# Second layer of a two-layer state-space kernel: state sums by fp32 transposes, softplus terms joined on TensorE, seven of 24 C-products on GpSimd

## The chip, the cores and the metric

The kernel runs on one core of one Trainium2 chip. The metric is the device time of a whole execution in microseconds (us); lower is better. Everything is fp32.

## The reference, cut to what matters

Two layers run one after the other on a tensor of 8 images, 192 channels and 64 x 64 pixels. The change touches the second layer alone, a bidirectional Mamba block on 8 sequences of 4096 tokens with 192 channels. It normalises the tokens, runs the function below twice (once on the channels in reverse order, with its own weights), and adds both results to the normalised tokens.

```python
xc, z = split(x @ in_w.T)                    # 384 channels each
xc = silu(causal_conv(xc, 4 taps) + conv_b)
dt, B, C = split(xc @ x_w.T)                 # 12, 16, 16
dt = softplus(dt @ dt_w.T + dt_b)            # 384 channels
A = -exp(A_log)                              # 384 x 16 states
h[t] = exp(dt[t] * A) * h[t-1] + (dt[t] * xc[t]) * B[t]
y[t] = sum over the 16 states of h[t] * C[t]
y = (y + D * xc) * silu(z)
return y @ out_w.T
```

## The kernel before, in words

The second layer works on blocks of 512 tokens. There are 8 sequences of 8 blocks, and each block is passed twice (index `i` 0 and 1, one per Mamba), so there are 128 **passes**. Channels lie on the 128 partitions, in three channel blocks `c`, and tokens on the free axis. The 16 states of a channel block are taken two at a time, so a pass has 24 **groups** (3 channel blocks, 8 groups each), and the main loop (L947) has one **slot** per group. I number slots 0 to 23 within a pass.

A group does this:

- `inputs` (L831, GpSimd): dt * xc times B, for two states, 128 x 1022. It is issued three slots ahead.
- `decays` (L836, ScalarE): two exponentials into a PSUM tile `da`, and a copy of the first column. It is issued two slots ahead. There are two `da` buffers of two banks each.
- `scan` (L845, VectorE): the recurrence as one scan over 1024 elements.
- `keep` (L850, ScalarE): the last state is saved.
- `weigh` (L853): the product with C. It runs on VectorE for most groups (I call these near) and on GpSimd for the groups listed in `FAR` (far). The scan of a far group writes SBUF.
- `sum` (L857, TensorE): two matmuls with the identity add the two states into the PSUM tile `yp` of the channel block, three slots later (near) or four (far). The channels stay on the partitions.

Everything else of a pass is spread over the slots in two lists: `before[n]` is issued ahead of the scan of slot n, `behind[n]` after the decays of slot n. Much of it already belongs to the next pass. `enter` projects the input, `convolve` does the four taps as matmuls with diagonal weights (L695), `gate` projects z (L706), `silu` changes ScalarE's function table twice, `low_rank` computes dt, B and C, `spread` sends B and C by DMA to all partitions. `step` (L736) forms the terms of softplus on ScalarE, in six operations. `refine` (L753) joins them in three GpSimd operations and forms dt * xc in a fourth. `head` (L766) prepares the first column and waits for dt * xc. `gated` (L785) multiplies z by `yp`; `project` (L788) multiplies by the output weights, and `add` (L810) adds the result up.

Each engine issues its instructions strictly in the order in which the program emits them, so an instruction that waits holds up all that stand behind it on its engine. TensorE results outside `yp` go to PSUM tiles of the tag `bank` (L557). There are two of these, and a third result has to wait until the reader of an older one is done. The readers are ScalarE copies and activations, and VectorE for `add` when `i` is 1.

The order in one slot is `before`, `inputs` of slot n+3, `scan`, `sum` of older groups, `weigh`, `keep`, `decays` of slot n+2, `behind` (L947 to L972).

Of the kernel before, what the change touches and what calls it, by code (L numbers as in the profile page):

```python
# [8 lines left out]
F32 = mybir.dt.float32  # L9
# [22 lines left out]
FAR = (0, 12, 15, 20)  # L32
# [507 lines left out]
def kernel(ctx: ExitStack, tc: tile.TileContext, mid, ln, mambas, out):  # L540
# [21 lines left out]
    eps = const.tile([P, 2], F32, name="eps")  # L562
    eps, minus_one = eps[:, 0:1], eps[:, 1:2]
    nc.gpsimd.memset(eps, 1e-5)
    nc.gpsimd.memset(minus_one, -1.0)
# [99 lines left out]
    class Pass:  # L665
# [40 lines left out]
        def gate(self, c):  # L706
            if self.z is None:
                self.z = p2.tile([P, NC, T], F32, tag="z", name=f"z_{self.tag}")
            nc.scalar.copy(self.z[:, c, :], self.in_proj(NC + c))
# [26 lines left out]
        def step(self, c):  # L736


            pd = bank(f"pd_{self.tag}_{c}")
            nc.tensor.matmul(pd, self.m.dt_w[:, c * P : (c + 1) * P], self.dbl[:DTR, :], start=True, stop=True)  # L740
            self.e, self.lg, self.w = (
                p2.tile([P, T], F32, tag=kind, bufs=1, name=f"{kind}_{self.tag}_{c}") for kind in ("e", "lg", "w")
            )
            d = p2.tile([P, T], F32, tag="dt", name=f"dt_{self.tag}_{c}")
            nc.scalar.activation(self.e, pd, AF.Abs, bias=self.m.dt_b[:, c : c + 1])
            nc.scalar.activation(d, pd, AF.Relu, bias=self.m.dt_b[:, c : c + 1])  # L746
            nc.scalar.activation(self.e, self.e, AF.Exp, scale=-1.0)
            nc.scalar.activation(self.lg, self.e, AF.Ln, bias=1.0)
            nc.scalar.activation(self.w, self.e, AF.Identity, bias=1.0)
            nc.scalar.activation(self.w, self.w, AF.Identity, bias=minus_one)  # L750
            self.dt.append(d)

        def refine(self, c, part):  # L753
            d = self.dt[c]
            if part == 0:
                nc.gpsimd.tensor_sub(self.e, self.e, self.w)  # L756
            elif part == 1:
                nc.gpsimd.tensor_add(self.lg, self.lg, self.e)
            elif part == 2:
                nc.gpsimd.tensor_add(d, d, self.lg)  # L760
            else:
                dtx = p2.tile([P, T], F32, tag="dtx", name=f"dtx_{self.tag}_{c}")
                nc.gpsimd.tensor_mul(dtx, d, self.xc[:, c, :])
                self.dtx.append(dtx)

        def head(self, c, part):  # L766


            d, state = self.dt[c], self.m.state[:, c, :]
            if part == 0:  # L770
                first = self.first[c] = p2.tile([P, NS], F32, tag="first", name=f"first_{self.tag}_{c}")
                nc.scalar.activation(first, self.b0, AF.Identity, scale=self.dtx[c][:, 0:1])
                if self.k:
                    self.rest = p2.tile([P, NS], F32, tag="rest", name=f"rest_{self.tag}_{c}")
                    nc.scalar.activation(self.rest, self.m.a[:, c, :], AF.Exp, scale=d[:, 0:1])
                nc.scalar.copy(d[:, 0:1], never)
            elif self.k:
                nc.gpsimd.tensor_mul(self.rest, self.rest, state)
                nc.gpsimd.tensor_add(self.first[c], self.first[c], self.rest)

        def accumulate(self, c):
            self.yp.append(ps.tile([P, T], F32, tag="yp", name=f"yp{c}_{self.tag}"))
            nc.tensor.matmul(self.yp[c], self.m.d_diag[:, c, :], self.xc[:, c, :], start=True, stop=False)

        def gated(self, c):  # L785
            nc.vector.tensor_mul(self.z[:, c, :], self.z[:, c, :], self.yp[c])  # L786

        def project(self, half):  # L788

            self.po = bank(f"po_{self.tag}_{half}", (P, 2, CM))  # L790
            for s in range(2):
                at = slice((2 * half + s) * P, (2 * half + s + 1) * P)
                for c in range(NC):
                    nc.tensor.matmul(
                        self.po[:, s, :],
                        self.z[:, c, at],
                        self.m.out_w[:, c, :],
                        start=(c == 0),
                        stop=(c == NC - 1 and self.i == 1),
                    )  # L800
                for i in range(2 if self.i == 0 else 0):
# [3 lines left out]
                        ident[:KM, :KM],  # L805
                        start=False,
# [13 lines left out]
    class Group:  # L820
# [36 lines left out]
        def sum(self):  # L857
            for n in range(NG):
                stop = self.g == GROUPS - 1 and n == NG - 1
                nc.tensor.matmul(self.p.yp[self.c], ident, self.hs[:, n, :], start=False, stop=stop)  # L860
# [12 lines left out]
    for n, p in enumerate(passes):  # L873
        for c, slot in enumerate((-7, 1, 9)):
# [3 lines left out]
            for part in range(4):  # L878
                at(before, n, slot + 4, p.refine, c, part)
            for part in range(2):  # L880
                at(before, n, slot + 4 + part, p.head, c, part)
        for half, slot in enumerate((5, 10)):
            at(behind, n + 1, slot, p.project, half)
            at(before, n + 1, slot + 2, p.add, half)
# [10 lines left out]
        for c, slot in enumerate((13, 14, 16)):  # L895
            at(before, n - 1, slot, p.gate, c)
# [17 lines left out]
    with tc.manual_schedule():  # L914
# [7 lines left out]
        for c in range(NC):  # L922
            first.enter(c)
            first.convolve(c, range(4))
            first.gate(c)
# [6 lines left out]
        for part in range(4):  # L932
            first.refine(0, part)
# [13 lines left out]
        for n in range(len(before)):  # L947
# [11 lines left out]
            for by, far in ((3, False), (4, True)):  # L959
# [91 lines left out]
```

## Time and profile before

The median of three runs is 16998.13 us (16997.56 to 17017.5). The profiled execution has a span of 16996.8 us from its first to its last instruction; the page gives no other time for it, and the fastest run is 0.8 us above that span.

| stretch | span us | PE busy | DVE busy | ACT busy | POOL busy |
|---|---|---|---|---|---|
| whole execution | 16996.8 | 15880.5 | 15268.1 | 11938.6 | 15164.6 |
| second layer's loop, from its first state sum (6073 to 16990 us) | 10917 | 10116.6 | 10276.0 | 8234.2 | 10435.7 |

PE is TensorE, DVE VectorE, ACT ScalarE, POOL GpSimd. The stretch of the second layer divided by 128 passes is 85.3 us a pass. "Busy" of PE counts pipelined matmuls with modelled ends, so it overstates how full PE is. In the lists of groups, "idle before" is the time in which an engine stood still just ahead of that group, with what ended the wait. In the timeline a bracket holds the same for one row: the idle time and what ended it.

| operation of the second layer | engine | count | mean ns |
|---|---|---|---|
| `inputs` L834 | POOL | 3072 | 2351 |
| `scan` L848, near / far | DVE | 2560 / 512 | 2286 / 2280 |
| `weigh` L855 | DVE / POOL | 2560 / 512 | 1222 / 2353 |
| `sum` L860 (two instructions for each fp32 matmul) | PE | 12288 | 603 |
| `decays` L840 | ACT | 6144 | 691 |
| softplus joins L756, L758, L760 | POOL | 384 each | 1274, 1268, 1268 |
| dt * xc L763 | POOL | 384 | 1268 |
| copy of a 128 x 512 PSUM tile, L709 | ACT | 384 | 579 |

### The profile page before, as it was taken

What the parts mean: (1) busy time and instruction counts of PE and PEld (TensorE: products, weight loads), DVE (VectorE), ACT (ScalarE), POOL (GpSimd) and SP (SyncE); (2) the same over time, 40 slices, a digit from 0 to 9 for tenths busy, and PEclk for the clock granted to TensorE, in tenths of its full rate; (3) what the DMA queues carried; (4) which work ended last, traced back from release to release, by engine and by line L of the source; (5) the groups of instructions that cost most, each with busy time, mean ns of one, the idle gap of its engine ahead of it and who ended that gap; (6) DMA issues with size and microseconds to landing.
All of it is one profiled execution on the core that took longest, in us unless ns stands there. A gap on an engine that the chain in (4) does not pass through costs nothing.

```text
span 16996.8 us, 151143 instructions
## 1 busy us (share of the span) xinstructions
PE 15880.5 (93%) x42192; PEld 6479.2 (38%) x42192; DVE 15268.1 (90%) x14474; ACT 11938.6 (70%) x25451; POOL 15164.6 (89%) x9955
## 2 busy tenths in 40 slices
PE   9999999999999989999999999999999999999998
PEld 2333333333333334444444444444444444444443
DVE  8888888888887779999999999999999999999999
ACT  5656666666666667777777777777777777777777
POOL 7787978778787779999999999999999999999999
PEclk8999999999999999999999999999999999999999
DMA  1001010010100022222222222222222222222222
GB/s 30 24 7 30 1 30 9 22 30 1 30 1 26 3 95 105 105 105 105 104 106 104 106 104 106 104 106 104 106 104 106 104 106 104 106 104 103 106 102 87
DMA packets 695389, 1247.33 MB, mean 73 GB/s; under 512 B 311768, under 2 KB 378672, under 8 KB 694544
## 3 DMA queue, kind: packets, MB, share of 16 engines
q1 hardware_dynamic: 694144, 1237.37, 19.9%
q8 instruction: 335, 5.49, 0.1%
q14 instruction: 510, 4.18, 0.1%
q10 hardware_dynamic: 400, 0.29, 0.0%
HBM read 1178.77 MB, written 58.72 MB: 73 GB/s over the span
## 4 chain that ended last, share of the span: by engine, by line
DVE 26%; ACT 9%; POOL 9%; issue 8%; DMA 8%; PE 5%; SPq 0%; DVEq 0%; POOLq 0%; ACTq 0%
DVE da L848 18%; DMA c_sb<-bc 7%; POOL hs L834 6%; ACT da L840 3%; DVE hs L855 3%; DVE hs L848 3%; PE yp L860 2%; PE dbl_ps L721 1%; POOL hs L855 1%; DVE z L786 1%; DMA b_sb<-bc 1%; ACT xc L713 1%; ACT L713 1%; POOL e L756 1%; ACT xt L650 1%
## 5 line engine op out<-in xcount | busy, mean ns | idle before, releaser
L834 POOL TENSOR_TENSOR hs<-dtx,b_sb 128x1022 f32<-128x1022 f32 x3072 | 7140.1, 2351 | 62.1 <-DMA b_sb<-bc 29.8
L848 DVE TENSOR_TENSOR_SCAN da<-da,hs 128x1024 f32<-128x1024 f32 x2560 | 5852.5, 2286 | 497.0 <-ACT hs L843 462.8
L860 PE MATMUL yp<-hs,ident 128*128 128x512 f32 x12288 | 5764.5, 603 | 47.9 <-POOL hs L855 25.4
L840 ACT ACTIVATE da<-dt,a 128x512 f32<-128x512 f32 x6144 | 4246.7, 691 | 435.9 <-DVE hs L848 257.5
L860 PEld LDWEIGHTS yp<-hs,ident 128*128 128x128 f32 x12288 | 2316.7, 193 | 3058.9 <-issue 2700.9
L855 DVE TENSOR_TENSOR hs<-da,c_sb 128x1024 f32<-128x1024 f32 x2560 | 3129.3, 1222 | 88.4
L237 PE MATMUL g<-xp,w_gate_sb 16*128 16x512 f32 x8640 | 1816.2, 658 | 60.4 <-ACT dx L310 51.6
L851 ACT COPY state<-da 128x2 f32<-128x2 f32 x2560 | 399.4, 156 | 1981.8 <-DVE hs L855 1972.8
L700 PE MATMUL pc<-xr,conv_diag 128*128 128x512 f32 x3072 | 1572.3, 642 | 170.4 <-ACT dt L746 151.9
L678 PE MATMUL pi<-xT,in_w 96*128 96x512 f32 x3072 | 1447.2, 597 | 79.3 <-ACT y L816 36.5
L263 DVE TENSOR_TENSOR q<-g,h 128x512 f32<-128x512 f32 x2016 | 1351.4, 684 | 115.5 <-PE g L237 70.0
L273 PE MATMUL q<-q,ident 128*128 128x512 f32 x2688 | 1333.5, 619 | 0.0
L283 ACT ACTIVATE rc<-g,eps 128x512 f32<-128x512 f32 x672 | 462.0, 687 | 1116.7 <-DVE g L278 1116.7
L313 POOL TENSOR_TENSOR dx<-dx,xc 128x512 f32<-128x512 f32 x768 | 1079.5, 1406 | 156.6 <-ACT dx L310 133.6
L848 DVE TENSOR_TENSOR_SCAN hs<-da,hs 128x1024 f32<-128x1024 f32 x512 | 1167.5, 2280 | 57.2 <-POOL hs L834 57.2
L855 POOL TENSOR_TENSOR hs<-hs,c_sb 128x1024 f32<-128x1024 f32 x512 | 1204.9, 2353 | 1.2 <-ACT state L851 1.2
L267 POOL TENSOR_TENSOR q<-q,q 128x512 f32<-128x512 f32 x672 | 852.7, 1269 | 196.5 <-DVE q L263 190.9
L237 PEld LDWEIGHTS g<-xp,w_gate_sb 16*128 16x128 f32 x8640 | 495.0, 188 | 1304.9 <-DVE q L263 394.3
L700 PEld LDWEIGHTS pc<-xr,conv_diag 128*128 128x128 f32 x3072 | 584.8, 198 | 1029.0 <-issue 660.8
L257 POOL TENSOR_TENSOR lam<-lam,xc 128x512 f32<-128x512 f32 x672 | 942.0, 1402 | 33.3 <-ACT lam L254 33.3
L278 DVE TENSOR_TENSOR g<-g,ab 128x512 f32<-128x512 f32 x1344 | 933.0, 694 | 22.8
L196 DVE SCALAR_TENSOR_TENSOR xc<-pi,dw_sb,xc 128x504 f32<-128x504 f32 (+3 forms) x1152 | 839.5, 736 | 98.4 <-POOL xc L162 63.8
(140 smaller groups left out, 22975.2 us busy)
## 6 DMA issues: line engine op xcount, KB each, us to landing
b_sb<-bc SPq DMA_DIRECT2D x1024, 512.0 KB, 9.0
c_sb<-bc SPq DMA_DIRECT2D x1024, 512.0 KB, 8.9
xin<-in_x_dram SPq DMA_DIRECT2D x192, 384.0 KB, 3.6
mid<-ot SPq DMA_DIRECT2D x128, 192.0 KB, 2.1
xt<-mid SPq DMA_DIRECT2D x64, 384.0 KB, 10.0
out_dram<-y SPq DMA_DIRECT2D x64, 384.0 KB, 2.6
bc<-dbl SPq DMA_DIRECT2D x128, 64.0 KB, 1.6
b<-bc SPq DMA_DIRECT2D x128, 8.0 KB, 7.3
```

The costliest lines, as they stand in the source:

```text
L237: nc.tensor.matmul(dst, self.wg[r, at, self.d, :], flat(self.xp[r, self.j]), start=True, stop=True)
L257: nc.gpsimd.tensor_mul(self.lam if self.j else self.hc, self.lam, direction(self.xc, self.d, self.j))
L263: nc.vector.tensor_mul(self.q[i], rows(self.g[i]), self.h[:, :, i : i + HW])
L273: nc.tensor.matmul(self.sum, ident, flat(term), start=(i == 0), stop=(i == 1))
L313: nc.gpsimd.tensor_mul(self.dx, self.dx, direction(self.xc, self.d, self.j))
L678: nc.tensor.matmul(pi, self.m.in_w[:, i, c * P : (c + 1) * P], self.tokens.xT[:, i, :], start=(i == 0), stop=(i == 1))
L700: nc.tensor.matmul(pc, self.m.conv_w[:, c, t, :], self.xr[c][:, t : t + T], start=(t == 0), stop=(t == 3))
L834: nc.gpsimd.tensor_mul(self.hs[:, :, 1:], dtx, self.p.b_sb[self.g][:, :, 1:])
L840: nc.scalar.activation(self.da[:, n, :], self.p.dt[self.c], AF.Exp, scale=self.p.m.a[:, self.c, at : at + 1])
L848: nc.vector.tensor_tensor_scan(h, da, hs, 0.0, ALU.mult, ALU.add)
L855: engine.tensor_mul(self.hs, self.h, self.p.c_sb[self.g])
L860: nc.tensor.matmul(self.p.yp[self.c], ident, self.hs[:, n, :], start=False, stop=stop)
```

## The change

The state sum turns the layout over. For each of the two states and each 128 tokens, `sum` uses the slice of `hs` as the stationary operand and the identity as the moving one, with the transpose flag, and accumulates in `yp`. So `yp` has tokens on the partitions and channels on the free axis. `gate` and `accumulate` produce z and D * xc in that layout. `gated` multiplies there, and a new part, `turn_back`, transposes z back for `project` and copies it with ScalarE. The normalised tokens that `project` adds use the transpose flag too.

The terms of softplus are no longer added on GpSimd. `join` adds them by four matmuls with the identity into a `bank` tile, and `refine` copies the result to dt with ScalarE before GpSimd forms dt * xc. `step` writes a fourth term `r` and changes a sign. `FAR` has seven slots instead of four. `gate` has four parts (by 128 tokens, 384 wide) at slots 12, 13, 14 and 16 instead of three at 13, 14 and 16, and the first half of `project` moves from slot 5 to 6.

```diff
-FAR = (0, 12, 15, 20)
+FAR = (0, 3, 6, 9, 14, 17, 22)
...
-        def gate(self, c):
+        def gate(self, s):
...
-            nc.scalar.copy(self.z[:, c, :], self.in_proj(NC + c))
+                self.z = p2.tile([P, T // P, CI], F32, tag="z", name=f"z_{self.tag}")
+            pi = bank(f"pz_{self.tag}_{s}", (P, CI))
+            for i in range(2):
+                nc.tensor.matmul(
+                    pi,
+                    self.tokens.xT[:, i, s * P : (s + 1) * P],
+                    self.m.in_w[:, i, CI:],
+                    start=(i == 0),
+                    stop=(i == 1),
+                )
+            nc.scalar.copy(self.z[:, s, :], pi)
...
+            nc.scalar.activation(e, pd, AF.Abs, bias=self.m.dt_b[:, c : c + 1])
+            nc.scalar.activation(r, pd, AF.Relu, bias=self.m.dt_b[:, c : c + 1])
+            nc.scalar.activation(e, e, AF.Exp, scale=-1.0)
+            nc.scalar.activation(lg, e, AF.Ln, bias=1.0)
+            nc.scalar.activation(w, e, AF.Identity, bias=1.0)
+            nc.scalar.activation(w, w, AF.Identity, bias=1.0, scale=-1.0)
+
+        def join(self, c):
+
+            self.pj = bank(f"pj_{self.tag}_{c}")
+            for i, term in enumerate(self.terms):
+                nc.tensor.matmul(self.pj, ident, term, start=(i == 0), stop=(i == 3))
+
+        def refine(self, c):
             d = p2.tile([P, T], F32, tag="dt", name=f"dt_{self.tag}_{c}")
...
+            nc.scalar.copy(d, self.pj)
             self.dt.append(d)
-
-        def refine(self, c, part):
-            d = self.dt[c]
-            if part == 0:
-                nc.gpsimd.tensor_sub(self.e, self.e, self.w)
-            elif part == 1:
-                nc.gpsimd.tensor_add(self.lg, self.lg, self.e)
-            elif part == 2:
-                nc.gpsimd.tensor_add(d, d, self.lg)
-            else:
-                dtx = p2.tile([P, T], F32, tag="dtx", name=f"dtx_{self.tag}_{c}")
-                nc.gpsimd.tensor_mul(dtx, d, self.xc[:, c, :])
-                self.dtx.append(dtx)
+            dtx = p2.tile([P, T], F32, tag="dtx", name=f"dtx_{self.tag}_{c}")
+            nc.gpsimd.tensor_mul(dtx, d, self.xc[:, c, :])
+            self.dtx.append(dtx)
...
         def accumulate(self, c):
-            self.yp.append(ps.tile([P, T], F32, tag="yp", name=f"yp{c}_{self.tag}"))
-            nc.tensor.matmul(self.yp[c], self.m.d_diag[:, c, :], self.xc[:, c, :], start=True, stop=False)
+            self.yp.append(ps.tile([P, T // P, P], F32, tag="yp", name=f"yp{c}_{self.tag}"))
+            for s in range(T // P):
+                nc.tensor.matmul(
+                    self.yp[c][:, s, :],
+                    self.xc[:, c, s * P : (s + 1) * P],
+                    self.m.d_diag[:, c, :],
+                    start=(s == 0),
+                    stop=False,
+                )
...
+        def turn_back(self, c):
+
+            pt = bank(f"pb_{self.tag}_{c}", (P, T // P, P))
+            z = self.z[:, :, c * P : (c + 1) * P]
+            for s in range(T // P):
+                nc.tensor.transpose(pt[:, s, :], z[:, s, :], ident)
+            nc.scalar.copy(z, pt)
...
                         self.tokens.xT[:, i, at],
                         ident[:KM, :KM],
+                        is_transpose=True,
...
         def sum(self):
             for n in range(NG):
-                stop = self.g == GROUPS - 1 and n == NG - 1
-                nc.tensor.matmul(self.p.yp[self.c], ident, self.hs[:, n, :], start=False, stop=stop)
+                for s in range(T // P):
+                    nc.tensor.matmul(
+                        self.p.yp[self.c][:, s, :],
+                        self.hs[:, n, s * P : (s + 1) * P],
+                        ident,
+                        is_transpose=True,
+                        start=False,
+                        stop=(self.g == GROUPS - 1 and n == NG - 1 and s == T // P - 1),
+                    )
...
             at(behind, n, slot, p.step, c)
-            for part in range(4):
-                at(before, n, slot + 4, p.refine, c, part)
+            at(behind, n, slot + 3, p.join, c)
+            at(before, n, slot + 4, p.refine, c)
             for part in range(2):
                 at(before, n, slot + 4 + part, p.head, c, part)
-        for half, slot in enumerate((5, 10)):
+        for c, slot in enumerate((13, 21, 29)):
+            at(behind, n, slot, p.turn_back, c)
+        for half, slot in enumerate((6, 10)):
             at(behind, n + 1, slot, p.project, half)
             at(before, n + 1, slot + 2, p.add, half)
...
-        for c, slot in enumerate((13, 14, 16)):
-            at(before, n - 1, slot, p.gate, c)
+        for s, slot in enumerate((12, 13, 14, 16)):
+            at(before, n - 1, slot, p.gate, s)
...
-            for by, far in ((3, False), (4, True)):
+            for by, far in ((4, True), (3, False)):
```

The parts of the first pass, which stand ahead of the loop, change in the same way.

## The prediction

> **What bounds the kernel now.** I read the page first: in the second layer (the stretch from 6073 to 16990 us, 128 passes of 85.29 us) VectorE and GpSimd are both nearly full. The line gives the stretch, its length, the busy time of PE, PEld, DVE, ACT and POOL, then the granted clock (0.97), the DMA share and GB/s.
>
> ```profile
> 6073.00:16990.00 10917.00, 10116.60 (x25245) 4497.95 (x25246) 10276.04 (x6638) 8234.23 (x18795) 10435.66 (x6263) 0.97 0.27 104
> ```
>
> Per pass that is VectorE 80.3, GpSimd 81.5, ScalarE 64.3. Then VectorE's timeline, to see how a slot is spent and where it stops:
>
> ```profile
> 10010.56 2.29 DVE L848 TENSOR_TENSOR_SCAN da<-da,hs 128x1024 f32<-128x1024 f32 x1
> 10014.02 2.29 DVE L848 TENSOR_TENSOR_SCAN da<-da,hs 128x1024 f32<-128x1024 f32 x1
> ...
> 10036.18 2.28 DVE L848 TENSOR_TENSOR_SCAN hs<-da,hs 128x1024 f32<-128x1024 f32 x1
> 10038.38 2.27 DVE L848 TENSOR_TENSOR_SCAN da<-da,hs 128x1024 f32<-128x1024 f32 x1
> ...
> 10049.17 2.30 DVE L848 TENSOR_TENSOR_SCAN da<-da,hs 128x1024 f32<-128x1024 f32 x1 [1.60 <-ACT hs L843]
> 10058.44 2.30 DVE L848 TENSOR_TENSOR_SCAN da<-da,hs 128x1024 f32<-128x1024 f32 x1 [2.25 <-ACT hs L843]
> ```
>
> A near slot lasts 3.46 us (first two rows), a far one 2.20 (next two). So VectorE needs 20 x 3.46 + 4 x 2.20 + 3.1 (gated, add, statistics) = 81.1 a pass; the rest is waiting, and the list of waits says for whom:
>
> ```profile
> DVE da L848 <- ACT hs L843: 462.8, 238, 2.6
> PEld pi L678 <- ACT y L816: 72.1, 62, 2.1
> PEld pi L678 <- ACT xc L704: 70.7, 64, 5.4
> ```
>
> First row: VectorE waits for ScalarE's decays, 462.8 / 128 = 3.62 us a pass. The next two tell what decides this case: TensorE stands still until ScalarE has read an older `bank` tile. With two such tiles the order of TensorE and ScalarE is one chain.
>
> **What is saved.** Three more products leave VectorE: 3 x (3.46 - 2.20) = 3.78 us a pass. GpSimd loses nine joins at 1.27 = 11.4 and gains three products at 2.353 = 7.1: 81.5 falls to 77.1. TensorE's matmuls of 512 columns follow each other at 0.43 us (four in 1.72). A transpose is much shorter:
>
> ```profile
> 10064.88 0.60 PE L657 MATMUL pt<-ident,xt 128*96 128x128 f32 x4
> 10065.32 1.88 PE L860 MATMUL yp<-hs,ident 128*128 128x512 f32 x4
> ```
>
> Four take 0.44, 0.11 each, with weights of 96 columns. Loads of 128 columns (L802) follow at 0.125 (four from 10097.72 to 10098.22), so 0.11 to 0.13; I take 0.11, since the sums move 128 columns as L657 does. The sums go from 96 x 0.43 = 41.3 to 192 x 0.11 = 21.1; `join` adds 24 x 0.43 = 10.3, `turn_back` 12 x 0.11 = 1.3, `accumulate` 24 x 0.17 (rate of L794's matmuls) - 6 x 0.43 = 1.5. Net -7 a pass: by these rates TensorE has (96 + 24 + 24 + 18) x 0.43 for sums, convolutions, projections and the rest of 512 columns, 24 x 0.17 for L794 and about 2 for L802 and L657, 75.8 before and 69 after (73 at 0.13). ScalarE gains three copies of dt and three of z at 0.58: 64.3 to 67.8. `gate` is as long as before (16 x 0.32 against 12 x 0.43), and the shorter transposes of L802 are worth under 1 us off the path. `project`'s first half and its add move by one slot together, so its bank is held no longer; the new order of far and near sums costs TensorE nothing, since both operands are there. The dropped constant is one memset of 0.1 us. If ScalarE's waits stayed at 3.62, a pass would take 81.5.
>
> **What it adds: waits.** ScalarE has a narrow margin. Per slot it needs 1.63 (keep and decays, 10042.42 to 10044.05), and its lateness shows on VectorE once the two-slot lead is used up. Behind a far slot the lead is 1.26 shorter. `join` (3.44 us of TensorE) stands in front of the second half of a convolution in slots 4 and 12, and ScalarE must wait for that convolution (L704), then for the copy of dt, then for a round trip to GpSimd (dtx 1.27 + 0.1; `head` needs it), before its next decays. Before, GpSimd did the joins in advance, and L772's wait for dtx was 107 us in all. I follow each place by rows of this trace.
>
> *Slots 11 to 15*, from the end of product 11. VectorE reaches scan 15 after add 0.54 + 3.46 + 3.46 + 2.20 = 9.7. ScalarE: decays 13 until 1.6. The first `gate`, now in slot 12, finds one bank held by the half-done convolution and the other by `project`, so it starts after the add (0.54), ends at 2.1, is copied by 2.6. `scale` (1.86) and decays 14 take ScalarE to 6.1. `join` needs the gate's bank: 2.6 + 3.44, then convolution 1.72 + 0.2 pipeline = 8.0. L704 to 8.6, dt copy 9.2, dtx 10.5, head 11.2, next gate copy 11.7, decays 15 done at 13.3. Wait 3.7. When `i` is 1 the add is a ScalarE copy, the gate is copied by 4.2, decays 15 are done at 14.9 against 9.1: 5.8. Mean 4.7; before: none here.
>
> *Slots 15 to 18*, from scan 15: copies 1.0, decays 16 at 2.6, decays 17 after product 15 at 5.1, gate and silu block 6.05 (10050.56 to 10056.61), decays 18 at 12.8. VectorE, slot 17 being far, is there at 9.1. Wait 3.7.
>
> *Slots 1 to 4*: decays 4 ended 12.7 after scan 0 began (10079.46 to 10092.17) behind `step`; VectorE now arrives at 11.8. Wait 0.9.
>
> *Slots 4 to 7*, from scan 4: L704 frees a bank at 0.6, `join` and convolution end at 6.0, L704 6.6, dt copy 7.2, dtx 8.6, head 9.2, decays 7 at 10.9. VectorE: 9.1. Wait 1.8.
>
> *Slots 20 to 23*: `join` is done in time; decays 22, turn, copy, dtx, head and decays 23 are 6.5 against 5.7, without the turn 5.8. Mean wait 0.5.
>
> Sum 4.7 + 3.7 + 0.9 + 1.8 + 0.5 = 11.6 in place of 3.62. The old 1.60 wait (scan 16) goes, with slot 15 no longer far; the silu wait grows. **A pass: 85.29 - 3.78 - 3.62 + 11.6 = 89.5**, +4.2, over 128 passes +540 us. On the span of 16996.8 that is 17,537; the runs lie about 1 us above the span, so **17,540 us**. What hides the cheap edits is the waiting itself: GpSimd (77) and TensorE are off this path, and GpSimd's three extra products run inside its own waits for the dt copy. Without that cover GpSimd's balance is 7.1 - 11.4 = -4.3, still a gain. DMA: no transfer is added; c_sb tiles of groups read by GpSimd come free one slot later, with 9 us to land (page, part 6) and six slots to spare.
>
> Bounds: each wait is a chain of measured pieces, but an engine's lead can shorten it. If every join is done when ScalarE arrives, only round trips and the far slots' shorter lead stay (about 6 us of waits, 84 a pass, 16,830). If pieces slip by another slot's ScalarE work in two places, +3.3: 17,960. This case's own range is 17,200 to 17,900.
>
> **A rule against the change.** The trace shows the clock falling after idle time:
>
> ```profile
> 10053.98 4.46 PE L721 MATMUL dbl_ps<-xc,x_w 128*44 128x512 f32 x6 [2.80 <-ACT xc L713]
> ```
>
> Six matmuls take 4.46 where 6 x 0.43 + 0.16 = 2.7 would do. In the eight transposes per two passes the trace cannot show what a long stretch of transposes does to the clock. The Trainium skill ("TensorE: Matmul & The Clock Gate", Part 4) says that transposes don't count as activity in the way matmuls do, so that the full clock isn't reached among them. By that rule slots 18, 19 and 21 to 23, which now hold hardly anything else, would run at half clock, and the estimate would be that of the second rival; by the 0.97 of the row above, nothing is added.
>
> **Rivals.** *Covered, faster.* TensorE leads ScalarE enough that joins are ready, and the balance of VectorE and GpSimd decides. For it: both were full, both are relieved, and `PE z L786` type waits are small (46 us). Against: the two-bank waits above. It decides if the waits are under 7.4 a pass (3.62 + 3.78). At 3.6 to 6.7 a pass takes 81.5 to 84.6: 16,510 to 16,910, middle 16,700. *Cold clock.* The joins in slots 4, 12 and 20 run at 0.86 a matmul, as the later ones of L721 did (weights loaded at 10055.68 and 10056.54): 3.4 more in each, two of them uncovered, with half of the convolutions: about +5 a pass, 18,180. It needs a clock clearly under 0.9 in the stage. *The transposes do not come out short* (two instructions each, 0.22, so that `sum` doesn't do what it says): 192 x 0.22 = 42 instead of 21, TensorE 90 a pass, a bound of its own beside the forecast's 89.5, some 17,600. The rows of L657 (512 instructions for 64 x 8 transposes) speak against it; it is counted in the forecast's range.
>
> **Chances.** Forecast 0.60, covered 0.27, near no change 0.05 (waits close to 7.4), cold clock 0.08. A measurement of this kernel can tell about 0.2%. Faster is the covered case, 0.27; same 0.05; slower 0.68. The range leaves out 0.1 on each side: the low end lies inside the covered case at 16,620, the high end at the slipped chain, 17,960.
>
> **What would show it.** VectorE's wait for L843 grows from 463 to about 1,480 us and falls on scans 4, 7, 15 and 18, each behind a far slot; ScalarE waits for TensorE at the convolution's activation in slots 4 and 12 and for dtx three times a pass; VectorE busy in the stage falls by 480, GpSimd by about 560; transposes at 0.11. Wrong, if waits stay near 463: then the joins were ahead of ScalarE, and the bank chain is the step that failed. Wrong in another way, if the granted clock drops below 0.9.

## The result and the profile after

The changed kernel takes 17868.1 us (median of four runs, 17853.87 to 17870.83), against 17003.23 us before on the same chip (four runs). The ratio is 1.0506, with a 95% interval of 1.0494 to 1.0519: slower by 5%. The forecast of 17,540 us had the sign and the chain of waits that makes the loss; the time lies 328 us above it, 2.6 us a pass.

The line for the second layer's stretch has the same columns as before: from and to, length, busy time of PE, PEld, DVE, ACT and POOL, then clock, DMA share and GB/s.

```profile
6073.00:17860.00 11787.00, 9665.10 (x44425) 6161.20 (x44426) 9870.44 (x6261) 8543.42 (x19695) 9998.48 (x5499) 0.92 0.26 96
```

The stretch is 870 us longer, and yet VectorE works 406 us less and GpSimd 437 us less. So no engine has become the bound by its work. The clock fell from 0.97 to 0.92. The list of waits of the stretch says who stands still for whom (time in all, times, longest):

```profile
engine line waited for: us in total, times, longest us
POOL dtx L770 <- ACT dt L767: 1666.9, 380, 11.3
...
DVE da L872 <- ACT hs L867: 940.7, 378, 8.6
DVE da L872 <- POOL rest L785: 691.8, 113, 8.9
ACT xc L702 <- PE pc L698: 640.2, 253, 6.8
...
ACT first L779 <- POOL dtx L770: 528.1, 382, 2.4
```

VectorE waits for decays in two rows (the second names a GpSimd operation that was done just before the decays it really waits for): 940.7 + 691.8 = 1632 us, where it had been 463 (a smaller row, put down to ScalarE's copy of the state as at scan 10 below, grew from 34 to 113). The other rows are the links in front of it. ScalarE waits for a convolution that stands behind a join, GpSimd for the dt that ScalarE copies from the join, and ScalarE again for GpSimd's product. VectorE's timeline shows two of its stops in a pass with `i` = 1, scans 10 and 15, each behind a far scan (`hs<-da,hs`):

```profile
12091.23 2.28 DVE L872 TENSOR_TENSOR_SCAN hs<-da,hs 128x1024 f32<-128x1024 f32 x1
12095.16 2.30 DVE L872 TENSOR_TENSOR_SCAN da<-da,hs 128x1024 f32<-128x1024 f32 x1 [1.65 <-ACT state L875]
...
12109.54 2.28 DVE L872 TENSOR_TENSOR_SCAN hs<-da,hs 128x1024 f32<-128x1024 f32 x1
12120.37 2.30 DVE L872 TENSOR_TENSOR_SCAN da<-da,hs 128x1024 f32<-128x1024 f32 x1 [8.55 <-ACT hs L867]
```

From the same records I took VectorE's idle time ahead of each scan, as a mean over passes 5 to 125:

| scan | forecast | measured, i = 0 | i = 1 | mean |
|---|---|---|---|---|
| 4 | 0.9 | 0.14 | 1.07 | 0.6 |
| 7 | 1.8 | 1.85 | 1.86 | 1.9 |
| 10 | 0 | 0.13 | 1.65 | 0.9 |
| 15 | 4.7 (3.7 and 5.8) | 3.72 | 8.73 | 6.2 |
| 18 | 3.7 | 3.63 | 3.65 | 3.6 |
| 23 | 0.5 | 1.67 | 0.35 | 1.0 |
| sum | 11.6 | | | 14.3 |

By the trace, a pass takes 92.19 us from scan to scan (85.39 before). The forecast's sum with the measured waits gives 85.39 - 3.78 - 3.92 + 14.3 = 92.0, so nearly the whole miss of 2.6 us a pass is in this column, and most of it in scan 15 when `i` is 1 (2.9 in half of the passes) and in scan 10.

The timeline around that stop, with the rows of the chain alone:

```profile
12104.36 0.47 ACT L840 COPY y<-po 128x384 f32<-128x384 f32 x1
...
12104.88 1.63 PE L710 MATMUL pz<-in_w,xT 96*128 96x384 f32 x4 [3.45 <-ACT y L840]
...
12107.08 2.08 PE L763 MATMUL pj<-r,ident 128*128 128x512 f32 x2 [0.57 <-ACT state L875]
...
12108.95 1.91 PE L763 MATMUL pj<-e,ident 128*128 128x512 f32 x2
...
12110.65 1.92 PE L763 MATMUL pj<-lg,ident 128*128 128x512 f32 x2
...
12112.36 1.38 PE L763 MATMUL pj<-w,ident 128*128 128x512 f32 x2
...
12115.49 0.69 ACT L702 ACTIVATE xc<-pc,vec_sb 128x512 f32<-128x512 f32 x1 [6.84 <-PE pc L698]
12116.08 0.58 ACT L767 COPY dt<-pj 128x512 f32<-128x512 f32 x1
...
12116.73 1.26 POOL L770 TENSOR_TENSOR dtx<-dt,xc 128x512 f32<-128x512 f32 x1 [11.29 <-ACT dt L767]
...
12118.03 0.31 ACT L779 ACTIVATE first<-b,dtx 128x16 f32<-128x16 f32 x1 [1.37 <-POOL dtx L770]
```

This is the forecast's chain link by link: add, gate, join, convolution, activation, dt, dtx, head. Only one link has another length. The terms of the join start 1.87, 1.70 and 1.71 apart, that is 0.86 an instruction and not 0.43. TensorE had stood still for 3.45 us at the gate just before; whether that is the cause is tested below. When `i` is 0, 61 of 64 of these joins go at 0.44 an instruction, and the wait is the forecast's 3.7.

### The profile page after: what moved, and what is told of

Its sections match the earlier page's. It is cut to its first block, busy times and chain, and to the rows that moved or that the text cites. A ratio compares the mean times of both kernels' runs of the same rounds, so it can differ in the third digit from the quotient of the medians.

```text
span 17867.8 us, 187845 instructions
## 1 busy us (share of the span) xinstructions
PE 15441.3 (86%) x61392; PEld 8143.5 (46%) x61392; DVE 14857.0 (83%) x14090; ACT 12245.6 (69%) x26347; POOL 14723.1 (82%) x9186
## 4 chain that ended last, share of the span: by engine, by line
POOL 34%; DVE 12%; issue 9%; ACT 5%; DMA 4%; PE 1%; SPq 0%; POOLq 0%; DVEq 0%; ACTq 0%
POOL hs L858 25%; POOL hs L879 7%; DVE da L872 6%; DMA c_sb<-bc 4%; DVE hs L872 3%; ACT da L864 2%; DVE hs L879 2%; POOL dtx L770 2%; ACT e L752 0%; ACT r L753 0%; ACT e L754 0%; PE pc L698 0%; ACT xc L721 0%; ACT z L722 0%; PE po L499 0%
## 5 line engine op out<-in xcount | busy, mean ns | idle before, releaser
L858 POOL TENSOR_TENSOR hs<-dtx,b_sb 128x1022 f32<-128x1022 f32 x3072 | 7282.2, 2395 | 32.0 <-DMA c_sb<-bc 1.5
L872 DVE TENSOR_TENSOR_SCAN da<-da,hs 128x1024 f32<-128x1024 f32 x2176 | 4985.3, 2291 | 1809.7 <-ACT hs L867 943.7
L884 PEld LDWEIGHTS yp<-ident,hs 128*128 128x128 f32 x24576 | 2954.6, 147 | 803.2 <-issue 491.6
L884 PE MATMUL yp<-ident,hs 128*128 128x128 f32 x24576 | 3185.1, 283 | 44.6 <-POOL hs L879 26.0
L879 DVE TENSOR_TENSOR hs<-da,c_sb 128x1024 f32<-128x1024 f32 x2176 | 2661.3, 1223 | 86.8
L879 POOL TENSOR_TENSOR hs<-hs,c_sb 128x1024 f32<-128x1024 f32 x896 | 2120.7, 2367 | 15.9 <-ACT state L875 15.9
L872 DVE TENSOR_TENSOR_SCAN hs<-da,hs 128x1024 f32<-128x1024 f32 x896 | 2042.2, 2279 | 60.2 <-POOL hs L858 54.8
L770 POOL TENSOR_TENSOR dtx<-dt,xc 128x512 f32<-128x512 f32 x384 | 487.3, 1269 | 1706.4 <-ACT dt L767 1706.4
L875 ACT COPY state<-da 128x2 f32<-128x2 f32 x2176 | 338.2, 155 | 1261.2 <-DVE hs L879 1252.7
L710 PE MATMUL pz<-in_w,xT 96*128 96x384 f32 x2048 | 820.2, 525 | 401.6 <-ACT y L840 220.4
L817 PE MATMUL po<-out_w,z 128*128 128x192 f32 x3072 | 726.6, 381 | 400.4 <-ACT z L809 400.4
L676 PE MATMUL pi<-xT,in_w 96*128 96x512 f32 x1536 | 758.7, 617 | 278.1 <-ACT z L809 210.2
```

The costliest lines, as they stand in the source:

```text
L858: nc.gpsimd.tensor_mul(self.hs[:, :, 1:], dtx, self.p.b_sb[self.g][:, :, 1:])
L872: nc.vector.tensor_tensor_scan(h, da, hs, 0.0, ALU.mult, ALU.add)
L879: engine.tensor_mul(self.hs, self.h, self.p.c_sb[self.g])
L884: nc.tensor.matmul(self.p.yp[self.c][:, s, :], self.hs[:, n, s * P : (s + 1) * P], ident, is_transpose=True, start=False, stop=(self.g == ...
```

## The experiments

Waits are again the mean idle time of VectorE ahead of a scan, and "a pass" is the mean distance of scan 0 from pass to pass. Ratios are against the kernel before on the same chip, which took 17,000 to 17,004 us (median) on each of them.

### Three parts alone

**Seven far groups alone**, in the kernel before.

```diff
-FAR = (0, 12, 15, 20)
+FAR = (0, 3, 6, 9, 14, 17, 22)
...
-            for by, far in ((3, False), (4, True)):
+            for by, far in ((4, True), (3, False)):
```

> The kernel before with only the list of far groups changed to the seven of the change (and far sums issued ahead of near ones, so that the last sum of a channel stays last). Three theories. CHAIN: the time of the change was lost because the join of softplus stands on TensorE and waits for one of two bank tiles, and ScalarE for it; then seven far products with the joins still on GpSimd show no wait at scans 4, 7 and 15 behind ScalarE's L702-like activation. What is left is GpSimd, 81.5 + 7.1 = 88.6 us a pass, which is now the bound, and the wait of scan 18 for silu, 3.6: about 89 a pass, 17,450. FAR: the seven far groups alone bring the loss; then 92 a pass, 17,850, with waits of scans 15 and 18 for ScalarE as after the change. CLOCK: transposes lower the clock; here there are none in the sums, so the granted clock stays at 0.96 to 0.97, and the time is GpSimd's, 17,450.

17635.95 us, ratio 1.0373 (1.0357 to 1.0388); 90.33 a pass.

```profile
6073.00:17640.00 11567.00, 10441.15 (x25260) 4664.12 (x25260) 9870.95 (x6263) 8191.90 (x18801) 11324.28 (x6650) 0.93 0.26 98
```

The line has the columns of before; GpSimd (the last busy time) works 11324 / 128 = 88.5 of 90.3 us: it is the bound, as CHAIN said, though the time is 1% over CHAIN's. Its lateness shows in ScalarE's wait for dtx, 964 us (102 before). Scans 7 and 15 wait too (2.8 and 3.2), and 4 and 10 a little (0.6 and 0.8), which CHAIN did not expect; the 964 us point to the same round trip, with GpSimd's own joins in place of the join on TensorE. The clock is 0.93, where CLOCK had 0.96 to 0.97: a fall of that size comes without one transposed sum.

**Transposed sums alone**: the kernel after, with the softplus terms joined on GpSimd as before and four far groups.

```diff
-            at(behind, n, slot + 3, p.join, c)
-            at(before, n, slot + 4, p.refine, c)
+            for part in range(4):
+                at(before, n, slot + 4, p.refine, c, part)
...
-FAR = (0, 3, 6, 9, 14, 17, 22)
+FAR = (0, 12, 15, 20)
```

> The kernel after with the softplus joins back on GpSimd and the four far groups of before: the transposed sums alone (with the turn-back of z and the gates in four pieces). CHAIN: no join on TensorE, so no wait at scans 4, 7 and 15 beyond 1 us; the waits of before at 16 and 18 stay, with up to 1 us more at 15 from the gate that stands in slot 12: 85.4 to 87 a pass, 17,000 to 17,200. CLOCK: the short transposes leave TensorE idle or uncounted for most of the time, the granted clock falls to 0.93 as after the change, every matmul piece on the path doubles at times, and the time is 17,300 or more. FAR: as before, 17,000.

17057.86 us, ratio 1.0033 (1.0020 to 1.0045); 85.81 a pass.

```profile
6073.00:17050.00 10977.00, 8536.65 (x41364) 5813.95 (x41365) 10300.32 (x6641) 8444.68 (x19312) 10555.75 (x6264) 0.88 0.28 103
```

PE's busy time falls by 1580 us, and the time hardly moves: TensorE was off the path. The wait of scan 16 shrinks from 1.60 to 0.2, and 0.4 to 0.9 come at 7, 14 and 15; CHAIN had only the one at 15. The clock is 0.88, lower than in any other kernel here, for 0.3% of the time. So CLOCK, as a loss everywhere, is out: here a mean granted clock says nothing, since TensorE has slack.

**Sums and joins on TensorE, four far groups.**

```diff
-FAR = (0, 3, 6, 9, 14, 17, 22)
+FAR = (0, 12, 15, 20)
```

> The kernel after with the four far groups of before: transposed sums and joins on TensorE, no further product on GpSimd. CHAIN: VectorE works 3.8 us a pass more than after the change, the waits at scans 4, 7, 10 and 23 (4.3 in all) go, because no far slot shortens the lead there, those at 15 (3.7 and 8.7) and 18 (3.6) stay: about 91 a pass, 17,750. FAR: the joins cost nothing by themselves, the waits fall back to about 4 a pass: 85.4, 17,000. CLOCK: as after the change less the far part, granted clock 0.93, about 88 a pass.

17830.89 us, ratio 1.0486 (1.0470 to 1.0502); 91.92 a pass, near CHAIN's 91. Scan 15 waits 5.7 and 7.5 (CHAIN: 3.7 and 8.7), scan 18 2.2, scan 14 1.4, which CHAIN did not have, and 4, 7, 10 and 23 nothing. The joins of slot 12 take 4.6 us on average here, partly at half clock, when `i` is 0 too. So the joins cost 91.92 - 85.81 = 6.1 us a pass where they stand, and the three products that go to GpSimd after that change nothing (+0.3): what they save is lost at the scans behind the far slots.

### The chain behind the join

**Convolutions ahead of the join.**

```diff
-        for c, slots in enumerate(((1, 2), (11, 12), (2, 4))):
+        for c, slots in enumerate(((1, 2), (11, 11), (2, 3))):
```

> The kernel after with the second half of two convolutions issued one slot earlier (slots 3 and 11), ahead of the join, so that the join finds a free bank and ScalarE's activation after the convolution no longer waits for the join. CHAIN: scan 7's wait of 1.85 falls under 0.5, scan 15's of 3.7 and 8.7 to about 1.2 and 3; scan 18's 3.6 stays. Together 5.4 us a pass: 87 a pass, 17,200. FAR: bank order is not the cause; the wait moves to another instruction of the same slots, within 1 us a pass of 92.2, 17,800. CLOCK: the join in slot 12 runs cold all the same when TensorE stood idle before it; scan 15 in passes with i = 1 stays over 6 and the time is about 17,550.

17434.66 us, ratio 1.0252 (1.0237 to 1.0268); 88.75 a pass. Scan 15 falls from 3.72 and 8.73 to 1.65 and 2.91, near what CHAIN said, and all 64 of the joins with `i` = 1 are warm:

```profile
11529.26 1.56 PE L710 MATMUL pz<-in_w,xT 96*128 96x384 f32 x4 [1.10 <-ACT xc L702]
11530.65 1.02 PE L763 MATMUL pj<-r,ident 128*128 128x512 f32 x2
11531.51 1.02 PE L763 MATMUL pj<-e,ident 128*128 128x512 f32 x2
```

TensorE now stood still for 1.10 us and not 3.45, and the terms start 0.86 apart. Scan 7, however, stays at 1.7, against CHAIN's 0.5, and with it CHAIN's 87 a pass is missed. The timeline of slots 4 to 7 shows why:

```profile
11501.05 1.02 PE L763 MATMUL pj<-w,ident 128*128 128x512 f32 x2
...
11501.90 2.41 POOL L879 TENSOR_TENSOR hs<-hs,c_sb 128x1024 f32<-128x1024 f32 x1
11502.81 0.57 ACT L767 COPY dt<-pj 128x512 f32<-128x512 f32 x1
11504.24 1.30 POOL L770 TENSOR_TENSOR dtx<-dt,xc 128x512 f32<-128x512 f32 x1
11504.52 2.28 DVE L872 TENSOR_TENSOR_SCAN hs<-da,hs 128x1024 f32<-128x1024 f32 x1
11505.57 0.31 ACT L779 ACTIVATE first<-b,dtx 128x16 f32<-128x16 f32 x1 [2.19 <-POOL dtx L770]
11506.84 1.42 ACT L864 ACTIVATE da<-dt,a 128x512 f32<-128x512 f32 x2 [0.48 <-DVE hs L872]
11508.45 2.30 DVE L872 TENSOR_TENSOR_SCAN da<-da,hs 128x1024 f32<-128x1024 f32 x1 [1.65 <-POOL first L786]
```

The join is done in time and dt is copied at once. But dtx stands on GpSimd behind the product of far group 3, and ScalarE waits 2.19 us for it. (In the kernel after, dt came later and that product was done by then.) Then the decays of group 7 wait once more, until the far scan 6 has ended (11504.52 + 2.28 = 11506.80). That second wait was in nobody's theory.

**Gates behind the join.**

```diff
-        for s, slot in enumerate((12, 13, 14, 16)):
+        for s, slot in enumerate((13, 14, 15, 16)):
```

> The kernel after with the four gates in slots 13 to 16 in place of 12, 13, 14, 16, so that the join of slot 12 does not stand behind a gate that waits for the add. COLD theory: in passes with i = 1 the join ran at half clock because TensorE had stood idle for 3.45 us at that gate; with the gate gone, the join starts warm and scan 15's wait falls from 8.73 to about 4, in passes with i = 0 from 3.72 to about 2: 3.4 us a pass less, 88.8, 17,430. CHAIN without COLD: the gate's own length (1.57 and the wait for the add) goes from the chain, the join stays at 6.5 us: scan 15 at 6 or more when i = 1, 17,650. Neither: the gate only moves, scan 18 takes the wait, 17,850.

17522.76 us, ratio 1.0305 (1.0287 to 1.0323); 89.62 a pass, between COLD's 88.8 and the next. Scan 15 waits 1.65 when `i` is 0 and 5.07 when it is 1. The passes with `i` = 1 split (the last one, which has no next pass to prepare, left out): in 44 of 63 the join is still cold (5.4 us and more) and the wait is 5.69, in 19 it is warm (3.7 us) and the wait is 3.72. A row of each kind:

```profile
11048.57 1.16 PE L763 MATMUL pj<-r,ident 128*128 128x512 f32 x2 [3.45 <-ACT y L840]
...
13559.04 1.12 PE L763 MATMUL pj<-r,ident 128*128 128x512 f32 x2 [2.52 <-ACT y L840]
```

In both kinds the join begins at the same place, 6.18 us after scan 11 on average, so a cold join costs 2.0 us of VectorE's time here, measured inside one run. And its kind goes with how long TensorE stood still just ahead of it: 3.45 us or more before each of the 44, 2.53 us or less before each of the 19, where the sums, the projection and the convolution ahead of it had ended later. In the kernel after, all 63 were cold.

### Who gets the decay buffer

The second wait leads to the program as it is built. The decays of a group behind a far one carry a wait for VectorE there, where others wait only for ScalarE itself (groups 5, 6 and 7 with far group 6):

```
L875 TensorCopy state1<-da_0_3_1_4_0              [waits DVE]
L864 Activation da_0_3_1_6_0<-dt                  [waits Activation]
...
L875 TensorCopy state1<-da_0_3_1_5_0              [waits DVE]
L864 Activation da_0_3_1_7_0<-dt                  [waits DVE]
```

The semaphores in the trace say the same: in the kernel after, the decays of group 6 wait for one that ScalarE raises and those of group 7 for one that VectorE raises. The value that it waits for is the far scan of group 6. My reading is that the builder, by its own order of events, holds the far scan's `da` to be free before `keep` of group 5 has freed the other. So the decays of group 7 overwrite the tile that scan 6 has been reading, and there is no lead at all. The same happens before the change at scan 16 alone, behind far group 15: its 1.60 us. The trace agrees: there ScalarE stands idle for 2.04 us, and the decays of group 16 begin 0.04 us after scan 15 has ended, in every pass, while behind the other three far groups they begin about 2 us before that scan ends. I made the two buffers strictly alternate.

```diff
-            self.da = psd.tile([P, NG, T], F32, tag="da", name=f"da_{self.tag}")
+            self.da = psd.tile([P, NG, T], F32, tag=f"da{self.g % 2}", bufs=1, name=f"da_{self.tag}")
```

> The kernel before, with the two decay buffers used strictly in turn (a tag for even groups and one for odd ones). In the built program the decays of the group behind a far one take the buffer that the far scan is still reading, so they begin only when that scan ends (here scan 16 behind far 15, 1.60 us a pass). BUFFER theory: this wait goes: 83.8 to 84.2 a pass, 16,800 to 16,850. CHAIN theory (waits come only from the join, the bank tiles and ScalarE's order): a buffer more or less in turn changes nothing, 17,000; the 1.60 us moves to scan 18.

In the kernel before: 16808.25 us, ratio 0.9884 (0.9869 to 0.9899); 83.83 a pass. The 1.60 is gone; scan 18 takes 0.3 of it back (2.54) and scan 7 another 0.3. BUFFER holds, to its number.

> The kernel after, with the two decay buffers used strictly in turn. In the built program of the change five groups of 24 (4, 7, 15, 18, 23 in one layer, 4, 7, 10, 15, 18 in the other) take the buffer of the far scan just before them. BUFFER: the waits that are nothing else go, scan 4 (mean 0.6), 10 (0.9) and 23 (1.0); scans 7, 15 and 18 keep most of theirs, because there ScalarE is late by itself: 2.5 to 3.5 a pass less, about 89 a pass, 17,450. CHAIN: every wait behind a far group is ScalarE's lateness; within 0.5 us a pass of 92.2, 17,800.

In the kernel after: 17771.24 us, ratio 1.0450 (1.0434 to 1.0466); 91.38 a pass, 0.8 less and not 2.5 to 3.5. Scan 4 falls to 0.35, 10 to 0.7 and 23 to 0.7, while 20 gains 0.1. Here CHAIN is nearer: at most of these places ScalarE is late by itself, and the wrong buffer hides behind that. Scan 7 keeps its wait (1.7 and 2.4) and scan 15 most of it (4.0 and 7.7).

### Everything placed anew

**Joins ahead.** Buffers in turn, and:

```diff
-            at(behind, n, slot + 3, p.join, c)
-            at(before, n, slot + 4, p.refine, c)
+            at(behind, n, slot + 2, p.join, c)
+            at(before, n, slot + 3, p.refine, c)
...
-        for c, slots in enumerate(((1, 2), (11, 12), (2, 4))):
+        for c, slots in enumerate(((1, 1), (12, 12), (2, 2))):
...
-        for s, slot in enumerate((12, 13, 14, 16)):
+        for s, slot in enumerate((13, 14, 15, 16)):
```

> The kernel after with buffers in turn, and with the join out of ScalarE's way: both halves of each convolution in one slot (1, 12, 2), join and copy of dt with the dtx product one slot earlier, first gate behind the join (gates in 13 to 16). The far groups stay. CHAIN and BUFFER together: waits at 4, 7, 10, 15 and 23 add up to under 1.5 a pass, scan 18's stays at 3.6 to 4, VectorE works 77.9: about 83 a pass, 16,700, faster than before. If seven far products themselves were the cause (FAR): GpSimd at 78 of 83 would not keep up, waits for inputs show, and the time stays over 17,000.

17005.06 us, ratio 1.0000 (0.9990 to 1.0009); 85.36 a pass. The losses of the change are paid back, but the forecast of 16,700 was missed: waits of 7.4 stay, 4.0 of them at scan 18 and the rest at 4, 8, 10, 11, 14 and 15. One cause is in its waits:

```profile
ACT dt L767 <- PE pj L763: 420.2, 280, 3.2
```

The copy of dt now catches the join before it is done: 420 us of ScalarE, where it was 0.2 after the change. Join and copy have kept their distance. But after the change the activation of a convolution behind the join stood between them in ScalarE's order and took the wait (640 us, L702); it stands elsewhere now, and its own wait is 108.

For the next kernel I counted ScalarE's work slot by slot. The decays of group n+2 can only begin when slot n is over, since they take its buffer; ScalarE's waits for VectorE's product (L875 behind L879, 1009 us in the run with the joins ahead) show it standing there. So its lead is one slot. From `keep` to the copy of the first column it needs 1.7 us (11501.18 to 11502.90 in the trace of the kernel with the convolutions ahead). A near slot of 3.46 leaves 1.7 us for other parts, a far one of 2.20 leaves 0.5. A far slot costs nothing only where ScalarE has nothing else to do and is not late from the slot ahead; that is the reasoning behind the next kernel.

**Replaced**: far slots at such places, and the parts moved to suit. Buffers in turn, and:

```diff
+FAR = (1, 6, 8, 13, 14, 15, 22)
...
+        for c, slots in enumerate(((-7, -5, -4, -2, -2), (1, 3, 4, 5, 5), (8, 10, 11, 13, 13))):
...                       # step, join, refine, both parts of head
+        for c, slot in enumerate((18, 21, 28)):                      # turn_back
+        for half, slot in enumerate((5, 9)):                         # project
...
+        for c, slots in enumerate(((1, 1), (13, 13), (2, 4))):       # convolve
+        for s, slot in enumerate((11, 12, 15, 16)):                  # gate
```

> The kernel after with buffers in turn and every part placed anew: far groups 1, 6, 8, 13, 14, 15, 22, so that a far slot stands where ScalarE has nothing but decays to do and two near slots (16, 17) stand over the silu block; joins in slots 3, 10, 19, gates in 11, 12, 15, 16, convolutions whole in 1 and 13. CHAIN and BUFFER: only scan 18's wait of about 2.6 is left, 79.5 to 80.5 a pass, 16,250 to 16,400. If the cold clock of TensorE or GpSimd's load is what holds the kernel up: no better than the run with the joins ahead, 16,700.

16371.54 us, ratio 0.9627 (0.9612 to 0.9641); 80.42 a pass. The stretch, and the first row of VectorE's waits for decays:

```profile
6073.00:16365.00 10292.00, 9217.66 (x44442) 5975.77 (x44442) 9812.68 (x6257) 8570.65 (x19695) 9964.04 (x5501) 0.95 0.29 110
```

```profile
DVE da L872 <- ACT hs L867: 301.1, 148, 2.4
```

Every engine's busy time is within 5% of what it was after the change, and the stretch is 1495 us shorter. VectorE waits 301 us for decays, nearly all at scan 18 (2.15 and 2.42). As CHAIN said, the work of the change was not too much; the places were wrong.

Three variants of this kernel undo one thing each.

```diff
-FAR = (1, 6, 8, 13, 14, 15, 22)
+FAR = (0, 12, 15, 20)
```

> The kernel with everything placed anew, but with the four far groups of before (0, 12, 15, 20): what three more products on GpSimd are worth once nothing else waits. CHAIN: three near slots for far ones, 3.8 us a pass more, less some of scan 18's wait: 83 to 84, 16,700 to 16,800, no better than the kernel before with its buffers in turn (16,808). FAR (the products gain nothing even when placed well, GpSimd only takes the place of VectorE): within 0.5 us a pass of 80.4, 16,370.

16809.12 us, ratio 0.9885 (0.9871 to 0.9900); 83.80 a pass. The three products are worth 83.80 - 80.42 = 3.4 us a pass once they stand well, of the 3.78 that the forecast counted. And it equals the kernel before with its buffers in turn (83.83): the transposes and the joins on TensorE save nothing by themselves. They make the room on GpSimd that the three products need.

```diff
-FAR = (1, 6, 8, 13, 14, 15, 22)
+FAR = (0, 3, 6, 9, 14, 17, 22)
```

> The kernel with everything placed anew, but with the far groups of the change (0, 3, 6, 9, 14, 17, 22): the same load on every engine, other slots. PLACE theory: a far slot gives its successor's decays 2.2 us in place of 3.46; behind slots 2 (step), 8 and 10, and at 17 under the silu block this is lost again as waits of scans 4, 11 and 18: 2 to 3.5 us a pass more than 80.4, 16,650 to 16,800. If only the load counts: 16,370.

16849.85 us, ratio 0.9910 (0.9893 to 0.9926); 84.09 a pass, 3.7 more than with the other list at the same load (PLACE had 2 to 3.5). The waits are back behind far slots: 3.76 at scan 18, 1.0 at 11, 0.6 at 4.

```diff
-            self.da = psd.tile([P, NG, T], F32, tag=f"da{self.g % 2}", bufs=1, name=f"da_{self.tag}")
+            self.da = psd.tile([P, NG, T], F32, tag="da", name=f"da_{self.tag}")
```

> The kernel with everything placed anew, with the decay buffers handed out by the program's builder again. In the built program three groups of 48 (7 in both layers, 14 in the first) then take the buffer of the far scan just before them. BUFFER: a wait of up to 1.67 us at scan 7 and in half of the passes at 14: 1 to 2.5 us a pass more, 16,500 to 16,700. If ScalarE is late there anyway or VectorE has other work in those slots: within 0.3 us a pass, 16,400.

16661.71 us, ratio 0.9799 (0.9785 to 0.9814); 82.72 a pass, 2.3 more. Scan 7 waits 1.21 and 1.65, scan 14 1.67 when `i` is 0: the groups that the built program had named. What was worth 0.8 in the crowded kernel is worth 2.3 here, since nothing else is late there.

## Why the prediction was right, and where it was not

- **What bounds the kernel**: right. With four far groups VectorE's own work sets the time (83.8 a pass with almost no waits but scan 18's, in two kernels that differ in most of TensorE's work).
- **What is saved, 3 x 1.26 = 3.78**: right in size, shown by the pair with four and seven far groups (3.4: VectorE's own work falls by 3.5 and the waits hardly differ, 2.7 and 2.8). VectorE's busy time was to fall by 480 us and fell by 406; the 384 products that left it make 469 (1.222 each), and the rest was not followed. GpSimd's fall was put at 560 us and is 437. The step left out that `inputs` would get slower: 2351 ns before, 2395 after, 3072 times, 135 us.
- **TensorE's work off the path, transposes at 0.11**: right, but for the one join below. These are rows of TensorE in the kernel after, the first at full, the second at half clock:

```profile
12140.92 1.91 PE L884 MATMUL yp<-ident,hs 128*128 128x128 f32 x16
...
12154.30 1.91 PE L884 MATMUL yp<-ident,hs 128*128 128x128 f32 x8
```

  Sixteen take 1.91, 0.11 each and the pipeline's end; eight at half clock take as long.
- **Slots 11 to 15**: right when `i` is 0 (3.7 forecast, 3.72 measured); for `i` = 1 the term was 5.8 and measured 8.73. The mis-sized piece is the join, put at 3.44 until the convolution behind it can start, and taking 5.8 on average over these passes (3.5 when it is warm). The forecast kept the cold clock as a rival with one condition for the whole stage ("a clock clearly under 0.9"). The stage stood at 0.92, and the cold clock still decided at this one place, because it is the one where TensorE waits 3.45 us just ahead of a link of the chain. With the 2.2 us between a cold and a warm join taken off in half of the passes, scan 15's mean would be about 5.1, by this estimate near the 4.7.
- **Slots 15 to 18**: right, 3.7 and 3.64, with the right cause: silu's block, with slot 17 far. With 16 and 17 near it is 2.15 to 2.54.
- **Slots 4 to 7**: right, number and chain (1.8 and 1.9). These are its last links in a pass with `i` = 0, whose scan 4 began at 12167.81:

```profile
12174.38 0.58 ACT L767 COPY dt<-pj 128x512 f32<-128x512 f32 x1
...
12175.04 1.27 POOL L770 TENSOR_TENSOR dtx<-dt,xc 128x512 f32<-128x512 f32 x1 [1.00 <-ACT dt L767]
...
12177.06 1.42 ACT L864 ACTIVATE da<-dt,a 128x512 f32<-128x512 f32 x2
```

  From scan 4, dt is copied at 7.2 and dtx done at 8.5 (forecast 7.2 and 8.6). What the forecast did not see stands right beside it: the decays of group 7 take the buffer of far scan 6, which ended at 12177.02, 0.04 us before they began. By either bound alone the wait is about as long. Freeing the bank leaves 1.7 (the run with the convolutions ahead), the buffers in turn leave 1.7 and 2.4.
- **Slots 1 to 4 and 20 to 23**: 0.9 and 0.5 forecast, 0.6 and 1.0 measured. The buffer stands here too, unseen: the decays of group 4, and of group 23 when `i` is 0, begin 0.03 us after the far scan ahead of them has ended.
- **The old wait of 1.60 at scan 16**: its going was forecast rightly, since slot 15 is no longer far. The cause, the buffer, was not seen. That is one part of why scan 10 was missed (0 forecast, 0.9 measured), where the trace of the kernel after has it too:

```profile
12092.57 0.15 ACT L875 COPY state<-da 128x2 f32<-128x2 f32 x1
12093.54 1.42 ACT L864 ACTIVATE da<-dt,a 128x512 f32<-128x512 f32 x2 [0.82 <-DVE hs L872]
```

  With the buffers in turn 0.7 of the 0.9 stays, so ScalarE is late there by itself as well.

- **The lead.** The forecast spoke of a two-slot lead of ScalarE. With two buffers it is one slot. The sums came out because they followed rows and not that figure.
- **The rivals.** "Covered, faster" (waits under 7.4) did not come about in this kernel, but its balance is real: with 7.4 left the time is equal to before (joins ahead), with 2.8 left it is 16,372. "The transposes do not come out short" is out.
- **The rule.** The Trainium skill ("TensorE: Matmul & The Clock Gate", Part 4) holds that transposes don't count as activity as matmuls do, so that the full clock isn't reached among them. In slots 18, 19, 21 and 22 of the kernel after, which the prediction named, 5006 of 5021 distances between neighbouring transposes of the sums are at the full rate (about 0.11) and 15 at the half rate (0.22). The measurement decides against the rule for fp32 here. But matmuls stand among them, the join in slot 19 above all, against the prediction's "hardly anything else". In the kernel with transposed sums alone there is no join: 4138 of 4156 such distances in slots 18 and 19 are still at the full rate, and only 176 of 455 in slots 21 and 22. So transposes do run at the full clock, and whether they would hold it by themselves is not shown.

What stays open: what makes TensorE's work ahead of the join end later in 19 of 63 passes of the run with the later gates, and how much of the 7.4 left in the run with the joins ahead each link holds.

## What to carry to other kernels

Where an in-order engine feeds the bound engine through two buffers, its lead is one step: a step made shorter must be put where the feeder has nothing else to do, or what is saved comes back as a wait one step later. Follow every moved part through all the queues on its round trip, and ask what stands ahead of it there. In the built program, check whose buffer each tile takes; a tile handed out by the builder's own order of events can tie a producer to the consumer just ahead of it.

## What the runs showed of the hardware

- The half-clock stretches last 3.4 us or a multiple of it: of the 501 in the kernel after, 360 last 3.4, 97 6.8 and 27 10.2. In the 3.4 us ahead of one in the second layer, TensorE had been idle for 2.7 us (median) in the kernel after, and for 1.8 us in the kernel with everything placed anew: it need not stand still for the whole of it.
- GpSimd's `inputs` take 2351 to 2355 ns in all three kernels whose sums stream `hs` past the identity, and 2380 to 2399 in all eleven with transposed sums, whichever engine joins the terms and however many groups are far. So it comes with the turned layout, in which `hs` is the operand that is loaded. The mechanism is not shown.
